# Mamba recurrence in a hybrid network: one more product with C on GpSimd, and the second step's input taken from SBUF

## The chip, the cores and the metric

The kernel runs on one core of a Trainium2 chip. The metric is the device time of one execution in microseconds, the median of several runs. The core has TensorE (PE in the profile, PEld for its weight loads), VectorE (DVE), ScalarE (ACT), GpSimd (POOL), and SyncE (SP), which issues most of the DMAs here. Each engine works through its own queue of instructions.

## What is computed

A batch of one image, 64 x 64 positions (4096 tokens) with 256 channels, goes through two layers: first a convolution and attention block, then a two-directional Mamba block with a small MLP, then a mixture of experts. The change lies in the Mamba part of the second layer. Its core, from the reference:

```python
dt = softplus(einsum('blr,dr->bld', dt, dt_proj_w) + dt_proj_b)
A = -exp(A_log)
dA = exp(dt[..., None] * A)
dBx = dt[..., None] * Bm[:, :, None, :] * xc[..., None]
def step(h, inp):
    dA_t, dBx_t, C_t = inp
    h = dA_t * h + dBx_t
    y = einsum('bds,bs->bd', h, C_t)
    return (h, y)
y = ys.transpose(1, 0, 2) + xc * Dp
y = y * silu(z)
return einsum('bld,ed->ble', y, out_proj_w)
...
fwd = _mamba(x, ...[0])
bwd = _mamba(x[:, ::-1, :], ...[1])
```

There are 512 inner channels with 16 states each, so 8192 recurrences over 4096 tokens in each direction.

## The kernel before, in words

`mamba_phase` cuts the tokens into 8 chunks of 512. A **step** i is one chunk in one direction, c, d = divmod(i, 2): even steps run forward, odd steps run backward (chunk 7 - c, read in reverse), so there are 16 steps. Step 1 works on chunk 7, which the attention phase leaves last; `start()` norms it into a tile `un`.

A step has 32 **slots** (`slots`, `SPS` = 32): four blocks e of 128 inner channels, in each four groups k of states, in each two halves j = 0 and 2. A slot handles 128 partitions x 2 x 512 elements. In the code n counts slots over all steps, and `at` = n % 32 is the place in the step. One slot takes these instructions:

- `inflow(n)` (L1726, GpSimd): dbx = dtxr times b. dtxr and dtr are tiles loaded by `load_dt` (L1473, SP) from a scratch in HBM, with each row broadcast; one pair serves four slots, and each has three buffers. dbx has three buffers too.
- `decay(n)` (L1716, ScalarE, two instructions): da = exp(dtr * A).
- `bring(n)` (L1764 on ScalarE, or L1762 on GpSimd at the places in `LONG`, which has 1): from step 2 on adds what the earlier chunk left to one column of dbx.
- `recur(n)` (L1739, VectorE): the scan, and then, unless the place is in `POOLED`, the product of the states with C (L1744, VectorE). At a place in `POOLED` the scan writes tile h directly, and `pooled(n)` does the product on GpSimd (L1749), issued one slot later.
- `keep(n)` (L1770, ScalarE): saves the last column as state.
- `sum_states(n)` (L1779, TensorE): for a pair of slots n and n + 1, four matmuls, each into its own strip of 32 partitions, add the products to y. At the first pair of a block a matmul with `skip` (L1777) opens y; the y tile has one buffer.
- `close(i, e)` (L1787, VectorE): after the last pair of a block, multiplies y with silu(z) into xc, and so frees y.

The order of the work is written by hand: the phase runs in `tc.manual_schedule`, and each engine's queue holds its instructions in the order in which the loop over slots issues them. In slot n the loop issues, in this order: a `carry` part at the places in `CARRY`, `inflow(n + 2)`, `keep(n - 1)`, `decay(n + 1)`, `bring(n + 1)`, `recur(n)`, loads, `pooled(n - 1)`, the sums that are due and `close`, then a step of `output(i - 1)` (L1488, matmuls that read what close wrote), the Silu of z at place 0 (L1854), a step of preparation, and a piece of a tail. So in slot 31 GpSimd gets the next step's inflow for place 1 and then, if 30 were in `POOLED`, the product of 30.

A pair is summed two slots after its first slot (j = 0). A pair whose first place is in `POOLED` = {4, 10, 12, 18, 28} is summed one slot later (j = 2). `close` of a block's last pair is issued in the first slot of the next block, right after that slot's scan and product.

The preparation of a step is a generator, `prepare(q)`, of 36 pieces: the input projection (L1300, reads u), copies out of PSUM (L1326 to L1334), the convolution in four groups (L1346, L1342), its Silu (L1350), the projection to dt, B and C (L1355 to L1361), softplus in several pieces (L1371 to L1395), the projection to z, and six pieces `dt_piece` on GpSimd that also store dt and dt * xc to HBM. Each slot issues one piece; the last five slots of a step (`AHEAD`) already begin with the step after the next. In step 0 another table, `LATE`, says how many pieces of `prepare(1)` each place issues, and `start()` still runs in its first slots. There step 1's input goes out to HBM (`ud[NCH - 1]`, L1631) and is loaded again by `load_u(1)` (L1309).

Of the kernel before, what the change touches and what calls it, by code (L numbers as in the profile page):

```python
# [1216 lines left out]
def mamba_phase(cx, early, w_in, w_x, w_out, w1, w2, x1d, ud, bcd, dtd, x2d, u2d, usum):  # L1217
# [12 lines left out]
    with ExitStack() as ctx:  # L1230
# [314 lines left out]
        def start():  # L1545


            got, xp = gots[0], early.xp
            x1 = tl.tile([P, CT, N], FP, name="x1", tag="a1b")
            nc.gpsimd.dma_start(out=x1, in_=x1d[NCH - 1])  # L1550
            un = tl.tile([P, CT, N], FP, name="un", tag="hn")
            norm = layer_norm(cx, tl, tl_psum, x1, un, nc.gpsimd)
            nc.scalar.copy(halo[0], xp[:, :, N : N + 3])
            xc = got["xc"] = pr.tile([P, ET, N], FP, name="xc", tag="xc")
            nc.scalar.activation(xc, xp[:, :, 0:N], AF.Silu)
            for d in range(2):
                nc.scalar.activation(aneg[d], cx.col(f"alog{d}", 0, ET * DS), AF.Exp)

                nc.vector.tensor_scalar(aneg[d], aneg[d], -1.0, -1e-30, ALU.mult, ALU.min)
            nx = DR + 2 * DS  # L1560
            pd = mm_psum()
            for e in range(ET):
                nc.tensor.matmul(pd[0:nx, :], wx[0][:, e, :], xc[:, e, :], start=e == 0, stop=e == ET - 1)
            xd = few()[0:nx, :]
            nc.scalar.copy(xd, pd[0:nx, :])
            nc.sync.dma_start(out=bcd[0], in_=xd[DR:nx, :])
            load_bc(0, 0)
            ex = early.wide("ex")[:, :, 0:N]
            dt = got["dt"] = sp.tile([P, ET, N], FP, name="dt", tag="dt")

            def soft(e):
                ps = mm_psum()
                nc.tensor.matmul(ps, wdt[0:DR, P * e : P * e + P], xd[0:DR, :], start=True, stop=True)
                nc.scalar.activation(ex[:, e, :], ps, AF.Abs, bias=cx.col("dtb0", e))
                nc.vector.tensor_scalar(dt[:, e, :], ps, cx.col("dtb0", e), 0.0, ALU.add, ALU.max)
                nc.scalar.activation(ex[:, e, :], ex[:, e, :], AF.Exp, scale=-1.0)

            def rest(e):

                rd = few()  # L1580
                nc.vector.tensor_scalar(rd, ex[:, e, :], -1.0, -1.0, ALU.mult, ALU.add)
                nc.vector.scalar_tensor_tensor(rd, rd, 1.0, ex[:, e, :], ALU.add, ALU.add)
                nc.vector.tensor_tensor(dt[:, e, :], dt[:, e, :], rd, ALU.add)

            def log(e):
                nc.scalar.activation(ex[:, e, :], ex[:, e, :], AF.Ln, bias=1.0)

            soft(0)
            rest(0)
            log(0)  # L1590
            for v in range(2):
                dt_piece(0, v, 0, ex, nc.vector)
            load_dt(0, 0, 0)
            load_dt(0, 0, 2)
            load_bc(0, 1)

            step(norm)
            step(norm)
            soft(1)
            step(norm)  # L1600
            soft(2)
            rest(1)
            soft(3)
            step(norm)
            inflow(0)
            decay(0)
            decay(1)
            rest(2)
            rest(3)
            step(norm)  # L1610
            load_bc(0, 2)
            zs = in_pair(0, ET)
            for e in range(1, ET):
                log(e)
            inflow(1)
            step(norm)
            load_bc(0, 3)
            yield

            for h in range(2):  # L1620
                z = sp.tile([P, 2, N], FP, name="z", tag="z", bufs=3)
                got.setdefault("z", []).append(z)
                for f in range(2):
                    nc.scalar.copy(z[:, f, :], zs[f])
                if h == 0:
                    zs = in_pair(0, ET + 2)
                    for v in range(2):
                        dt_piece(0, v, 1, ex)
                    yield
            step(norm)  # L1630
            nc.sync.dma_start(out=ud[NCH - 1], in_=un)  # L1631
            drain(norm)
            yield
            dt_piece(0, 0, 2, ex)
            yield
            dt_piece(0, 1, 2)
            yield
            for z in got["z"]:
                nc.scalar.activation(z, z, AF.Silu)
            dt_piece(0, 0, 3, ex)  # L1640
            load_u(1)
            yield
            dt_piece(0, 1, 3)
            yield
# [59 lines left out]
        SPS = ET * SQ * 2  # L1704
# [67 lines left out]
        def sum_states(n):  # L1772

            i, e, k, _ = slots[n]
            if k == 0:
                ys[i, e] = py.tile([P, N], FP, name="y", tag="y")
                nc.tensor.matmul(ys[i, e], skip[i % 2][:, e, :], gots[i]["xc"][:, e, :], start=True, stop=False)  # L1777
            for j in range(4):
                nc.tensor.matmul(  # L1779
                    ys[i, e][32 * j : 32 * j + 32, :], cx.sel, hs[n + j // 2][:, j % 2, :],  # L1780
                    start=False, stop=k == SQ - 1,
                )
            del hs[n], hs[n + 1]
# [6 lines left out]
        CARRY = {30: (0, 0), 31: (0, 2), 9: (1, 0), 11: (1, 2)}  # L1790


        POOLED = {4, 10, 12, 18, 28}

        AHEAD = 5

        LATE = {0: 0, 1: 0, 2: 0, 3: 0, 4: 0, 6: 2, 7: 6, 13: 2, 14: 2, 15: 2, 16: 2}
        LONG = {1, 9, 17, 24}

        FULL = {  # L1800
# [7 lines left out]
        with tc.manual_schedule(engines=ORDERED):  # L1808
# [5 lines left out]
            for n, (i, e, k, j) in enumerate(slots):  # L1814
                at = n % SPS
                if at == 0:
                    prep, coming = coming, None
                if at in CARRY and 1 < i + (at > 16) < 2 * NCH:
                    carry(i + (at > 16), *CARRY[at])
                inflow(n + 2)  # L1820
                if n > 0:
                    keep(n - 1)
                if n > 0:
                    decay(n + 1)
                bring(n + 1)
                recur(n)
                nxt = (i, e + 1) if e < ET - 1 else (i + 1, 0)
                if nxt[0] < 2 * NCH:
                    if e == ET - 1 and j == 0:
                        load_bc(i + 1, k)  # L1830
                    if (k, j) == (1, 2):
                        load_dt(*nxt, 0)
                    if (k, j) == (2, 2):
                        load_dt(*nxt, 2)
                if n > 0 and (n - 1) % SPS in POOLED:
                    pooled(n - 1)
                if j == 2 and n > 2 and (n - 3) % SPS in POOLED:
                    sum_states(n - 3)
                if j == 0 and n > 0:
                    if (n - 2) % SPS not in POOLED:  # L1840
                        sum_states(n - 2)
                    if k == 0:
                        close(*slots[n - 2][:2])
                        if e == 0:
                            out = output(i - 1)
                if 1 <= at <= 3 and out is not None:
                    step(out)
                    if at == 3:
                        out = None
                        if (i - 1) % 2:  # L1850
                            tails.append(tail((i - 1) // 2))
                if at == 0 and i > 0:
                    for z in gots[i]["z"]:
                        nc.scalar.activation(z, z, AF.Silu)  # L1854
                if i == 0:
                    step(begin)
                step(prep, LATE.get(at, 1) if i == 0 else 1)
                if at >= SPS - AHEAD and i + 2 < 2 * NCH:
                    coming = coming or prepare(i + 2)
                    step(coming)  # L1860
                if i > 0 and at in (2, 4):
                    dt_piece(i, 1, 2 if at == 2 else 3)
                if at == 1 and i > 1:
                    load_first(i, 1)
                elif at in (10, 30) and 1 < i + (at > 16) < 2 * NCH:
                    carry(i + (at > 16), at < 16, 1)
                if i == 2 * NCH - 1 and at in (26, 28):
                    ending = ending or last_output()
                    step(ending)
                if tails and (i == 2 * NCH - 1 or at not in FULL[needs[0]]):  # L1870
                    needs[0] = next(tails[0], None)
                    if needs[0] is None:
                        tails.pop(0)
                        needs[0] = "PE"
# [331 lines left out]
```

## Time and profile before

| what | value |
|---|---|
| median of 3 runs | 4168.57 us (4154.93 to 4173.5) |
| the profiled execution | 4163.05 us |
| its span, first to last instruction | 4160.9 us |
| mean granted TensorE clock | 0.923 |
| busy: PE, DVE, ACT, POOL | 3614.7, 3492.5, 2662.8, 1747.6 us |
| first scan of the Mamba recurrence to the last close | 1971.2 to 3837.9 us |
| step 0, first scan to the first scan of step 1 | 124.2 us |
| step 1 and 2, likewise | 110.5 and 114.2 us |
| steps 3 to 14, likewise | 113.5 to 119.1 us |

How to read it: a group's row on the page has line, engine, operation, output<-inputs, shapes and count, then busy time in us and mean of one in ns, then the idle time of that engine just before these instructions and what ended most of it. A timeline row has its start in us from the start of the span, its duration, engine, line and what it does; in brackets the idle time before it and its releaser. A row of the waits has who waited for whom, then the sum in us, the number of times, and the longest.

### The profile page before, as it was taken

The numbers are of one execution on the slowest core, as the hardware profiler recorded it, in microseconds if no ns is written. First come the engines' busy times: TensorE is split into PE (matmuls) and PEld (weight loads), VectorE is DVE, ScalarE is ACT, GpSimd is POOL, SyncE is SP. The second block draws the span as 40 slices with busy tenths as digits, with TensorE's granted clock in tenths as the row PEclk, the third lists the DMA queues.
The fourth block names the chain that finished last, engine by engine and source line by source line (L and its number), as shares of the span: only waits on it lengthen the run. The fifth ranks groups of instructions, "written<-read, shape, count | busy, mean of one in ns | idle before, by whom it ended". The sixth has DMA issues, their size and how long they took to land. (4 is left out here: it accounts for less than half of the span.)

```text
span 4160.9 us, 43567 instructions
## 1 busy us (share of the span) xinstructions
PE 3614.7 (87%) x15116; PEld 1185.4 (28%) x15116; DVE 3492.5 (84%) x2898; ACT 2662.8 (64%) x4131; POOL 1747.6 (42%) x1188
## 2 busy tenths in 40 slices
PE   6669789999999999998788788888888888876798
PEld 2223332222222222222222222222222222222343
DVE  8998867889889888778899999999999999998211
ACT  1111226878878878776777778778787877774122
POOL 3020000000000000001888889888898989896000
PEclk9889898999999999999888988998899999987899
DMA  6232124000000000002334344343334334341121
GB/s 207 91 110 94 56 71 135 12 27 19 19 21 19 19 22 19 11 22 86 110 117 126 121 126 129 117 133 112 125 115 124 120 122 141 108 137 64 66 67 39
DMA packets 150533, 351.20 MB, mean 84 GB/s; under 512 B 35493, under 2 KB 44453, under 8 KB 150046
## 3 DMA queue, kind: packets, MB, share of 16 engines
q1 hardware_dynamic: 139214, 313.17, 24.4%
q0 software_dynamic: 11088, 35.14, 2.4%
q8 instruction: 121, 1.98, 0.2%
q14 instruction: 110, 0.90, 0.1%
HBM read 268.69 MB, written 79.56 MB: 84 GB/s over the span
## 5 line engine op out<-in xcount | busy, mean ns | idle before, releaser
L1726 POOL TENSOR_TENSOR dbx<-dtxr,b 128x1024 f32<-128x1024 f32 x512 | 1202.1, 2358 | 192.9 <-DMA dtxr<-dtd 92.4
L1010 ACT ACTIVATE e<-sc 128x1024 f32<-128x1024 f32 x1024 | 992.9, 1023 | 203.4 <-PE sc L1003 160.3
L1739 DVE TENSOR_TENSOR_SCAN da<-da,state,dbx 128x1024 f32<-128x1024 f32 x432 | 1014.2, 2348 | 17.9 <-ACT da L1716 8.4
L929 DVE TENSOR_TENSOR s<-s,e 128x1024 f32<-128x1024 f32 x768 | 881.0, 1223 | 43.3 <-ACT e L1010 42.8
L1716 ACT ACTIVATE da<-dtr,aneg 128x512 f32<-128x512 f32 x1024 | 708.2, 692 | 33.2 <-DMA dtr<-dtd 3.3
L1003 PE MATMUL sc<-q,kS 32*128 32x512 f32 x4096 | 654.0, 643 | 11.7 <-ACT e L1010 7.8
L132 POOL TENSOR_TENSOR ln_few<-ln_few,minus_half 128x4 f32<-128x4 f32 x29 | 29.4, 1015 | 1408.1 <-DMA ln_few<-ln_row 1408.1
L1744 DVE TENSOR_TENSOR h<-da,c 128x1024 f32<-128x1024 f32 x432 | 529.2, 1225 | 34.0 <-PE y L1779 2.1
L936 PE MATMUL av<-e,vT 128*32 128x512 f32 x4096 | 548.7, 607 | 3.7 <-ACT o L942 3.7
L1779 PE MATMUL y<-h,sel 128*32 128x512 f32 x2048 | 373.2, 655 | 99.1 <-DVE h L1744 71.5
L453 PE MATMUL cv<-v,u 128*128 128x512 f32 x928 | 409.0, 600 | 28.0 <-DVE pad L274 14.3
L1300 PE MATMUL mm<-u,win 128*128 128x512 f32 x496 | 271.7, 699 | 88.1 <-ACT state L1770 29.1
L1003 PEld LDWEIGHTS sc<-q,kS 32*128 32x128 f32 x4096 | 211.7, 184 | 456.3 <-issue 229.8
L551 DVE SCALAR_TENSOR_TENSOR acc<-pad,wdw_s,acc 128x768 f32<-128x768 f32 (+1 forms) x192 | 235.9, 1234 | 25.6 <-ACT acc L544 20.0
L453 PEld LDWEIGHTS cv<-v,u 128*128 128x128 f32 x928 | 176.7, 192 | 258.4 <-issue 224.6
L1770 ACT COPY state<-da 128x2 f32<-128x2 f32 x431 | 68.0, 158 | 264.3 <-DVE h L1744 263.2
L1346 PE MATMUL mm<-xp,taps 128*128 128x512 f32 x480 | 213.2, 596 | 0.0
L929 DVE TENSOR_TENSOR s<-e 128x1024 f32<-128x1024 f32 x128 | 151.1, 1224 | 64.3 <-ACT e L1010 64.0
L1739 DVE TENSOR_TENSOR_SCAN h<-da,state,dbx 128x1024 f32<-128x1024 f32 x80 | 187.5, 2344 | 11.6 <-ACT state L1770 10.9
L936 PEld LDWEIGHTS av<-e,vT 128*32 128x32 f32 x4096 | 81.2, 108 | 396.4 <-issue 378.7
L1749 POOL TENSOR_TENSOR h<-h,c 128x1024 f32<-128x1024 f32 x80 | 188.4, 2355 | 2.1 <-ACT state L1770 2.1
L1300 PEld LDWEIGHTS mm<-u,win 128*128 128x128 f32 x496 | 106.2, 224 | 254.4 <-issue 109.8
(352 smaller groups left out, 3841.4 us busy)
## 6 DMA issues: line engine op xcount, KB each, us to landing
dtr<-dtd SPq DMA_DIRECT2D x128, 512.0 KB
dtxr<-dtd SPq DMA_DIRECT2D x128, 512.0 KB
b<-bcd SPq DMA_DIRECT2D x64, 256.0 KB
c<-bcd SPq DMA_DIRECT2D x64, 256.0 KB
dtd<-dt SPq DMA_DIRECT2D x64, 256.0 KB
dtd<-few SPq DMA_DIRECT2D x64, 256.0 KB
u<-uv SPq DMA_DIRECT2D x24, 640.0 KB
u<-ud SPq DMA_DIRECT2D x16, 512.0 KB
```

Source lines behind the costliest of these rows:

```text
L453: nc.tensor.matmul(rows4(ps), u[:, dy, P * ci : P * ci + P], v[:, dy : dy + HR, ci, :], start=dy + ci == 0, stop=dy == k - 1 and ci == CT - 1,
L551: nc.vector.scalar_tensor_tensor(o, src, w_ap, o, ALU.mult, ALU.add)
L929: nc.vector.tensor_tensor(z, x, y, ALU.add)
L936: nc.tensor.matmul(g.av[32 * h : 32 * h + 32, :], vT[:, kb, P * t + 32 * h : P * t + 32 * h + 32], es[h // 2][:, h % 2, :], start=kb == 0, ...
L1003: nc.tensor.matmul(ps[h // 2][:, h % 2, :], kS[r, t, P * kb : P * kb + P], q_t[r, t, :], start=True, stop=True,)
L1010: nc.scalar.activation(e, ps[i], AF.Exp)
L1300: nc.tensor.matmul(ps, win[d][:, t, P * e : P * e + P], u[:, t, ::-1] if d else u[:, t, :], start=t == 0, stop=t == CT - 1,)
L1716: nc.scalar.activation(da[:, v, :], dts[i, e, j][0][:, v, :], AF.Exp, scale=aneg[i % 2][:, a : a + 1])
L1726: nc.gpsimd.tensor_tensor(u, dts[i, e, j][1], bcs[i, k][0][:, None, :].to_broadcast([P, 2, N]), ALU.mult)
L1739: nc.vector.tensor_tensor_scan(das[n].rearrange("p v n -> p (v n)"), da.rearrange("p v n -> p (v n)"), u.rearrange("p v n -> p (v n)"), st ...
L1744: nc.vector.tensor_tensor(h, da, bcs[i, k][1][:, None, :].to_broadcast([P, 2, N]), ALU.mult)
L1779: nc.tensor.matmul(ys[i, e][32 * j : 32 * j + 32, :], cx.sel, hs[n + j // 2][:, j % 2, :], start=False, stop=k == SQ - 1,)
```

## The change

Step 1's input is taken from the tile `un` where the norm leaves it (`gots[1] = {"u": un}`), and `load_u(1)` goes. The store of that chunk to `ud` stays, since step 14 reads it. `LATE` starts `prepare(1)` at place 4 instead of 5; at places 4 to 16 the pieces lie up to two earlier or one later than before (16 issued by place 13 in both), and from place 17 on as before.

Place 30 joins `POOLED`: in every step, slot 30's product with C goes from VectorE to GpSimd. Its sum is not put off by a slot: where the first slot of a block (k == 0) is reached, the sum is issued at once, as `close` follows. The condition of the sums that are put off is written accordingly. In every sum the two strips of slot n + 1 are now added before those of slot n.

```diff
@@ start()
             norm = layer_norm(cx, tl, tl_psum, x1, un, nc.gpsimd)
+            gots[1] = {"u": un}
...
             dt_piece(0, 0, 3, ex)
-            load_u(1)
             yield
@@ sum_states(n)
-            for j in range(4):
+
+            for j in (2, 3, 0, 1):
                 nc.tensor.matmul(
                     ys[i, e][32 * j : 32 * j + 32, :], cx.sel, hs[n + j // 2][:, j % 2, :],
@@ tables
-        POOLED = {4, 10, 12, 18, 28}
+        POOLED = {4, 10, 12, 18, 28, 30}
...
-        LATE = {0: 0, 1: 0, 2: 0, 3: 0, 4: 0, 6: 2, 7: 6, 13: 2, 14: 2, 15: 2, 16: 2}
+        LATE = {0: 0, 1: 0, 2: 0, 3: 0, 5: 2, 6: 2, 7: 5, 15: 2, 16: 2, 17: 2}
@@ the loop over slots
-                if j == 2 and n > 2 and (n - 3) % SPS in POOLED:
+                if j == 2 and k > 0 and (n - 3) % SPS in POOLED:
                     sum_states(n - 3)
                 if j == 0 and n > 0:
-                    if (n - 2) % SPS not in POOLED:
+                    if k == 0 or (n - 2) % SPS not in POOLED:
                         sum_states(n - 2)
                     if k == 0:
                         close(*slots[n - 2][:2])
```

## The prediction

> **What bounds the kernel now.** I read the page first (busy times, then the groups), then the busy times by stretches of the Mamba phase (the recurrence, 1971 to 3840 us of the span), then the waits of each engine there, and last the timeline around a change of step. The page's groups give the price of one of each:
>
> ```profile
> L1726 POOL TENSOR_TENSOR dbx<-dtxr,b 128x1024 f32<-128x1024 f32 x512 | 1202.1, 2358 | 192.9 <-DMA dtxr<-dtd 92.4
> L1739 DVE TENSOR_TENSOR_SCAN da<-da,state,dbx 128x1024 f32<-128x1024 f32 x432 | 1014.2, 2348 | 17.9 <-ACT da L1716 8.4
> L1744 DVE TENSOR_TENSOR h<-da,c 128x1024 f32<-128x1024 f32 x432 | 529.2, 1225 | 34.0 <-PE y L1779 2.1
> L1749 POOL TENSOR_TENSOR h<-h,c 128x1024 f32<-128x1024 f32 x80 | 188.4, 2355 | 2.1 <-ACT state L1770 2.1
> ```
>
> 512 slots: each has one scan on VectorE (2.35 us); 432 have their product with C there (1.23), 80 on GpSimd (2.36). The stretches (columns: length, then busy time and count of PE, weight loads, VectorE, ScalarE, GpSimd, clock, DMA share, GB/s), each about one step of 32 slots:
>
> ```profile
> 2555.00:2670.00 115.00, 96.76 (x265) 31.31 (x268) 109.05 (x67) 90.95 (x180) 101.98 (x64) 0.88 0.40 120
> 3475.00:3590.00 115.00, 98.16 (x273) 31.96 (x274) 111.99 (x68) 94.35 (x186) 105.95 (x65) 0.88 0.40 122
> ```
>
> VectorE is busy 109 to 112 of 115 us, the rest is mostly gaps of some 0.03 to 0.1 us between instructions: it sets the step. GpSimd, at 102 to 106, is close behind. In its waits VectorE loses little; the largest are 14.1 us in step 0, from slot 5 to slot 16. The waits of 1970 to 2048 us say from where:
>
> ```profile
> DVE da L1739 <- ACT da L1716: 8.4, 4, 2.8
> DVE xc L1787 <- PE y L1779: 3.8, 2, 3.2
> PE mm L1300 <- DMA u<-ud: 7.0, 1, 7.0
> ```
>
> TensorE stands 7.0 us for step 1's input, then its work is late, ScalarE waits for it, and VectorE for ScalarE. The timeline where step 4 ends and step 5 begins:
>
> ```profile
> 2544.08 2.36 POOL L1749 TENSOR_TENSOR h<-h,c 128x1024 f32<-128x1024 f32 x1
> ...
> 2546.11 0.60 SPq L1473 DMA_DIRECT2D dtxr<-dtd  x1
> ...
> 2547.58 1.23 DVE L1744 TENSOR_TENSOR h<-da,c 128x1024 f32<-128x1024 f32 x1
> ...
> 2548.06 2.36 POOL L1726 TENSOR_TENSOR dbx<-dtxr,b 128x1024 f32<-128x1024 f32 x1
> ...
> 2551.17 1.23 DVE L1744 TENSOR_TENSOR h<-da,c 128x1024 f32<-128x1024 f32 x1
> ...
> 2552.45 1.05 PE L1779 MATMUL y<-h,sel 128*32 128x512 f32 x4 [1.11 <-DVE h L1744]
> 2552.50 2.36 POOL L1726 TENSOR_TENSOR dbx<-dtxr,b 128x1024 f32<-128x1024 f32 x1 [1.90 <-DVE h L1744]
> ...
> 2554.75 1.23 DVE L1744 TENSOR_TENSOR h<-da,c 128x1024 f32<-128x1024 f32 x1
> 2554.94 0.19 POOL L1762 TENSOR_TENSOR dbx<-dbx,brought 128x1 f32<-128x1 f32 x1
> 2555.08 6.99 POOL L1726 TENSOR_TENSOR dbx<-dtxr,b 128x1024 f32<-128x1024 f32 x3
> ...
> 2555.89 0.68 DVE L1787 TENSOR_TENSOR xc<-y,z 128x512 f32<-128x512 f32 x1
> 2556.49 2.35 DVE L1739 TENSOR_TENSOR_SCAN da<-da,state,dbx 128x1024 f32<-128x1024 f32 x1
> ```
>
> The first line is slot 28's product on GpSimd. The product of slot 30 is VectorE's at 2547.58, that of 31 at 2551.17. GpSimd's inflow for slot 0 of step 5 runs at 2548.06, that for slot 1 only at 2552.50: its tile dtxr was asked for at 2546.11, 6.4 us earlier. (The trace names a VectorE product as releaser; but this inflow's buffer was read last by slot 30's scan, long over, so I take the tile's landing.) At 2555.89 close (L1787) takes y, before the scan of slot 1.
>
> **What the Trainium skill says.** "PSUM — Partial Sum Buffer", Engine vs sequencer instructions: the queues of ScalarE, VectorE and GpSimdE are strictly first in, first out. The trace agrees: every inflow and product stands in the order of the code. "GPSIMD Engine Reference", 4.1 Engine selection: an elementwise operation of two inputs is about half as fast there; here 2355 against 1225 ns, 1.92 times. "ScalarE: Activation LUTs", What ACT_TABLE_LOAD costs: about 1283 ns for the load, and a drain of 1380; the trace has the 1.28 us, but the Silu at 2026.05 starts 1.29 us after its load's start at 2024.76, so no drain is counted.
>
> **The change, part by part.**
>
> 1. Slot 30's product leaves VectorE in 16 steps. A slot with product takes 3.59 us from scan to scan (2548.72 to 2552.32 is 3.60), one without 2.26 (2539.36 to 2541.62); I count 1.25 to 1.3, so at most 16 x 1.3 = 21 us.
>
> 2. What the same product does on GpSimd. pooled(30) is issued in slot 31, after that slot's inflow(n + 2), which is the one for slot 1 of the next step, and its bring (L1762). So it starts not when slot 30's scan ends (about 2547.5) but after 2555.1. Its sum isn't put off by a slot as those of the other five are: close comes at once. On VectorE close stands ahead of the scans of the whole next step, so they wait for the product. End of the product = end of inflow(1) + 0.24 (L1762 and gaps; none into step 1) + 2.36. Then 1.2 us to close: 1.06 for a sum on TensorE and two hand-overs (in step 0 a sum starts at 2009.03 and close at 2010.18). For step 5: 2554.86 + 0.24 + 2.36 + 1.2 = 2558.7, against 2555.89 before and 2554.64 with the gain of 1.25: VectorE stands 4.0 us and close is 2.8 us later than before. To the scan of slot 2 it is 0.61 + 3.59 us: 2562.9. Before it ran at 2560.39, after 0.28 us for ScalarE, which is no longer late then. So 2.5 us are lost. The same sum for all 15 changes of step, into step 1, 2, ... 15, from the trace's inflow, close and slot 2 scan: 0.0, 4.2, 4.2, 3.6, 2.5, 2.5, 1.2, 3.4, 1.4, 0.4, 3.3, 2.1, 2.8, 3.9, -0.1: together **+35.4 us**, the saving on VectorE already taken off. Where inflow(1) waited for nothing (steps 1, 10, 15) the loss is 0 to 0.4; elsewhere it waited 0.8 to 5.1. I take it that these repeat: from slot 23 on GpSimd runs without a pause (2520.55 to 2550.6, 0.2 us idle), released by a load that follows VectorE's pace.
>
> 3. The last slot 30 has no inflow behind it: its 2.36 us lie beside slot 31's scan and product (3.57): -1.3 us.
>
> 4. GpSimd after the change of step: 2.36 us later, VectorE as late, so no new wait there: 0. TensorE holds behind the sum of slot 30 the output's first three matmuls (L1488), which now run before close (2553.43, 2.84 us). It comes out at product's end + 6.8 (sum and hand-over 1.15, L1488 3.6, skip 1.0, slot 0's sum 1.05) = 2564.3, before 2561.2: 3.1 us later, VectorE 2.5. Its conv and ScalarE's Silu behind that gave waits of 1.3 to 1.6 us at slot 12 of steps 5, 6, 8, 10, 12 and 14. Between 0 and 0.6 a step; I take 0.2: +3.
>
> 5. Step 0. The norm's last multiply leaves `un` at 2.34 us from 1979.84, 1982.2; the copy out to ud and load_u(1) (issued 1990.27, used 1994.3) fall from the way of TensorE, which can start after its sum at 1987.3: 7 us sooner. By hand through the new LATE: the wait of 2.77 at slot 8 goes; close of slot 8 still waits, since two conv groups (3.7 us each) stand before its sum, and comes near 2007.3 for 2010.18; Silu moves to slot 11, in front of the decay of slot 13, while slot 12 has only its scan: some 3.5 us for the 2.40 there before; the 2.36, 0.86 and 0.56 at slots 14 to 16 go; one step more of ScalarE work in 15 to 17 may bring 1.5 back. Left: **-4**. Bounds: 0, and -12.2 (all but the 1.95 at slots 5 and 6, which the z Silu makes). SP has one issue (0.39 us) less; its queue isn't late there. `un` lies in a buffer that the next tail takes two steps later: 0.
>
> 6. The order 2, 3, 0, 1 in a sum: the product that may be late is used last. A sum takes about 1.05 us whether 2 or 4 of its matmuls are left (the x4 and x8 rows): 0; if four late ones cost 0.9 more (one sum took 1.9) at the 6 closes that waited, +5. The two conditions move no other sum: the old five pairs are put off as before.
>
> Sum: 35.4 - 1.3 + 3 - 4 = +33 us. On the profiled execution, 4163.05 us (span 4160.9 and 2.15 around it), that is 4196; the median of the runs, 4168.57, lies 5.5 above it, which gives 4202. I say **4199**.
>
> **The rivals.** (a) Faster: the product is hidden. If GpSimd has finished inflow(1) 3.8 us before the new close, nothing waits: 16 x -1.3 - 4 = -25, 4138 to 4144. For it: VectorE is the bound and GpSimd has 9 us a step to spare. Against it: the best three changes of step still miss by 1.6 to 2.1 us (0.3 to 0.8 us lost at close, plus the 1.25). (b) No change: GpSimd's queue sets the close, but the loads land in time everywhere, as into steps 1, 10 and 15: 15 x 0.3 - 1.3 - 4 = -1, 4165. (c) Worse: TensorE, held behind the sum, makes conv, Silu and decay late, and each step loses 0.6 there instead of 0.2 and another 1.5 at slots 12 and 16, as several do now: 33 + 15 x 1.9 = 61, 4224 to 4230.
>
> **Chances.** Forecast 0.66, (a) 0.10, (b) 0.16, (c) 0.08. 0.5% (21 us; about what a measurement can tell from no change) ends at 4189: of the forecast's own range, 4178 to 4218 by the unknowns above, about 0.09 lies below. So faster 0.10, same 0.25, slower 0.65. The range 4163 to 4225 leaves out (a), a part of (b) and of (c).
>
> **What would show it.** L1744 x416 and L1749 x96; VectorE's wait at L1787 for y rises from 10.9 to some 65 us, about 4 at the first close of a step, with GpSimd's L1749 just before it, behind an L1726 that waited for dtxr; TensorE's 7.0 us on u<-ud gone and step 0 (124.2 us to the first scan of step 1) near 119. I am wrong if L1787's wait stays near 10, or if the steps from 1 on are 1.3 us shorter.

## The result, and the profile after

The changed kernel takes 4208.24 us, median of 4 runs (4202.44 to 4215.9); the kernel before, with one more run beside it, 4167.23. The medians differ by 41 us; the ratio on record, taken over the runs, is 1.0109, 95% interval 1.009 to 1.0128. The forecast was 4199, from a working that came to 33 us more. The profiled execution has a span of 4204.2 us.

The rows of the page that answer to those of before:

```profile
L1726 POOL TENSOR_TENSOR dbx<-dtxr,b 128x1024 f32<-128x1024 f32 x512 | 1203.2, 2359 | 196.5 <-DMA dtxr<-dtd 97.5
L1739 DVE TENSOR_TENSOR_SCAN da<-da,state,dbx 128x1024 f32<-128x1024 f32 x416 | 976.5, 2347 | 19.6 <-ACT dbx L1764 11.5
L1744 DVE TENSOR_TENSOR h<-da,c 128x1024 f32<-128x1024 f32 x416 | 509.6, 1225 | 31.0 <-PE y L1780 0.7
L1749 POOL TENSOR_TENSOR h<-h,c 128x1024 f32<-128x1024 f32 x96 | 226.0, 2355 | 1.4 <-ACT state L1770 1.4
```

Sixteen products moved, 1225 ns each on VectorE and 2355 on GpSimd. One scan (2347 ns) and one product on VectorE take as long as before (2348 and 1225), so the sixth product beside them doesn't slow them. VectorE's busy time on the page fell from 3492.5 to 3474.2 us, 18 us. It stands longer than that for something new. VectorE's waits of 1960 to 3890 us:

```profile
DVE xc L1788 <- PE y L1780: 65.3, 20, 9.2
DVE h L1739 <- ACT state L1770: 18.1, 19, 1.6
DVE da L1739 <- ACT dbx L1764: 11.5, 12, 1.7
```

`close` (now L1788) waits 65.3 us for y, where it waited 10.9. From VectorE's timeline, 56.2 of it is the first close of the steps 1 to 15, which had no wait before. The timeline at the same change of step as before, step 4 to 5, with the releaser in brackets. The first line is slot 28's product, the next the issue of the load that slot 1's inflow waits for, the third slot 30's scan:

```profile
2563.77 2.37 POOL L1749 TENSOR_TENSOR h<-h,c 128x1024 f32<-128x1024 f32 x1
...
2564.80 0.60 SPq L1473 DMA_DIRECT2D dtxr<-dtd  x1
2564.81 2.34 DVE L1739 TENSOR_TENSOR_SCAN h<-da,state,dbx 128x1024 f32<-128x1024 f32 x1
...
2567.77 2.37 POOL L1726 TENSOR_TENSOR dbx<-dtxr,b 128x1024 f32<-128x1024 f32 x1
...
2571.06 2.35 POOL L1726 TENSOR_TENSOR dbx<-dtxr,b 128x1024 f32<-128x1024 f32 x1 [0.74 <-DMA dtxr<-dtd]
...
2573.13 1.23 DVE L1744 TENSOR_TENSOR h<-da,c 128x1024 f32<-128x1024 f32 x1
...
2573.49 0.19 POOL L1762 TENSOR_TENSOR dbx<-dbx,brought 128x1 f32<-128x1 f32 x1
2573.63 2.35 POOL L1749 TENSOR_TENSOR h<-h,c 128x1024 f32<-128x1024 f32 x1
...
2576.04 1.57 PE L1780 MATMUL y<-h,sel 128*32 128x512 f32 x4 [4.21 <-POOL h L1749]
...
2577.54 4.83 PE L1488 MATMUL mm<-xc,wout 128*128 128x512 f32 x8
2577.65 0.69 DVE L1788 TENSOR_TENSOR xc<-y,z 128x512 f32<-128x512 f32 x1 [3.29 <-PE y L1780]
```

Slot 30's scan ends at 2567.15. Its product starts at 2573.63, behind two inflows and a bring; the second inflow waited for its dtxr tile, asked for at 2564.80. The sum on TensorE waits 4.21 us for the product, close 3.29 us for the sum, and close stands before the scan of slot 1. Each wait is charged to the engine just before it; the first cause lies further back, in what stands ahead of the product in GpSimd's queue. At this change of step most of the delay is the two inflows and what else GpSimd had before them, and the load adds 0.74 us; at the change from step 2 to 3 the second inflow waited 6.3 us for its load.

### The profile page after: what moved, and what is told of

Same layout as the page of the kernel before. It is cut to its first block, busy times and chain, and to the rows that moved or that the text cites. A ratio compares the mean times of both kernels' runs of the same rounds, so it can differ in the third digit from the quotient of the medians.

```text
span 4204.2 us, 43522 instructions
## 1 busy us (share of the span) xinstructions
PE 3602.9 (86%) x15116; PEld 1185.8 (28%) x15116; DVE 3474.2 (83%) x2882; ACT 2661.5 (63%) x4131; POOL 1786.3 (42%) x1204
## 5 line engine op out<-in xcount | busy, mean ns | idle before, releaser
L1739 DVE TENSOR_TENSOR_SCAN da<-da,state,dbx 128x1024 f32<-128x1024 f32 x416 | 976.5, 2347 | 19.6 <-ACT dbx L1764 11.5
L1716 ACT ACTIVATE da<-dtr,aneg 128x512 f32<-128x512 f32 x1024 | 708.2, 692 | 46.4 <-DVE h L1739 12.6
L1744 DVE TENSOR_TENSOR h<-da,c 128x1024 f32<-128x1024 f32 x416 | 509.6, 1225 | 31.0 <-PE y L1780 0.7
L1780 PE MATMUL y<-h,sel 128*32 128x512 f32 x2048 | 341.3, 668 | 175.2 <-DVE h L1744 96.8
L1300 PE MATMUL mm<-u,win 128*128 128x512 f32 x464 | 249.9, 688 | 76.4 <-ACT z L1407 26.0
L1739 DVE TENSOR_TENSOR_SCAN h<-da,state,dbx 128x1024 f32<-128x1024 f32 x96 | 225.0, 2344 | 18.8 <-ACT state L1770 18.1
L1749 POOL TENSOR_TENSOR h<-h,c 128x1024 f32<-128x1024 f32 x96 | 226.0, 2355 | 1.4 <-ACT state L1770 1.4
L1770 ACT COPY state<-da 128x2 f32<-128x2 f32 x415 | 65.3, 157 | 245.1 <-DVE h L1744 244.0
L1780 PEld LDWEIGHTS y<-h,sel 128*32 128x32 f32 x2048 | 48.6, 112 | 420.5 <-DVE h L1744 181.6
```

What stands on the lines that cost most here:

```text
L1300: nc.tensor.matmul(ps, win[d][:, t, P * e : P * e + P], u[:, t, ::-1] if d else u[:, t, :], start=t == 0, stop=t == CT - 1,)
L1716: nc.scalar.activation(da[:, v, :], dts[i, e, j][0][:, v, :], AF.Exp, scale=aneg[i % 2][:, a : a + 1])
L1739: nc.vector.tensor_tensor_scan(das[n].rearrange("p v n -> p (v n)"), da.rearrange("p v n -> p (v n)"), u.rearrange("p v n -> p (v n)"), st ...
L1744: nc.vector.tensor_tensor(h, da, bcs[i, k][1][:, None, :].to_broadcast([P, 2, N]), ALU.mult)
L1780: nc.tensor.matmul(ys[i, e][32 * j : 32 * j + 32, :], cx.sel, hs[n + j // 2][:, j % 2, :], start=False, stop=k == SQ - 1,)
```

## The experiments

All ratios are to the kernel before on the same chip, with their intervals. My theory (1): the product is late because it stands behind an inflow that waits for its load, and close stands behind the product. The rivals: (2) GpSimd has no room for a sixth product; (3) the new order within the sums costs; (4) the step 0 part disturbs the later steps.

**One part at a time.** First the step 0 part alone:

```diff
+            gots[1] = {"u": un}
...
-            load_u(1)
...
-        LATE = {0: 0, 1: 0, 2: 0, 3: 0, 4: 0, 6: 2, 7: 6, 13: 2, 14: 2, 15: 2, 16: 2}
+        LATE = {0: 0, 1: 0, 2: 0, 3: 0, 5: 2, 6: 2, 7: 5, 15: 2, 16: 2, 17: 2}
```

> The kernel before with the step 0 part alone: un as step 1's input, no load_u(1), the new LATE; POOLED and the sums as before. My theory: step 0 is 4 to 6 us shorter (118 to 120 us from its first scan to that of step 1, 124.2 before), nothing else moves: about 4162, some 5 us under the kernel before; the wait at close in slot 0 of the steps stays near zero. Rival (the step 0 part shifts the later steps): steps 1 to 15 longer, over 4175.

4154.95 us, ratio 0.9993 (0.9983 to 1.0004). Step 0 took 120.0 us instead of 124.2; steps 1 to 14 took 116.1 us on average, before 115.9. So in the profile this part takes some 4 us off step 0 and leaves the later steps as they were, and rival (4) falls; the time as a whole can't be told from that of the kernel before.

Then the other part alone, the changed kernel with that diff undone:

> The changed kernel without its step 0 part: load_u(1) and the old LATE, un not used as input; place 30 and the new order in the sums stay. My theory: step 0 about 124 us from its first scan to that of step 1 where the changed kernel has 118.6; the rest as in the changed kernel with 50 to 60 us at close in slot 0: 3 to 6 us over the changed kernel, 1.011 to 1.013 times the kernel before. Rival: the two parts act on each other (the early preparation makes the later steps slow): under 1.005.

4200.42 us, 1.0097 (1.0075 to 1.0118); step 0 took 125.9 us, and the first closes waited 52.4 us. The loss is there without the step 0 part. The 3 to 6 us that this part was expected to save don't show: the medians even differ the other way, and each of the two ratios is uncertain by 8 or 9 us.

Then the changed kernel with the old order of the strips:

```diff
-            for j in (2, 3, 0, 1):
+            for j in range(4):
```

> The changed kernel with the strips of a sum added in the old order 0, 1, 2, 3. Theory 1: the order costs nothing, within 5 us of the changed kernel (1.009 to 1.012 times the kernel before), with 50 to 60 us at close in slot 0. Theory 3 (the new order costs): under 1.005.

4206.89 us, 1.0125 (1.0105 to 1.0146), 57.5 us at the first closes. Without the new order the loss is as large, so the order isn't what costs; whether it gains a little can't be told, since the intervals overlap. Rival (3) falls.

**Take away the load's wait.** The inflow for slot 1 reads the earlier dtxr tile. The values of slot 1 are wrong then; what is looked at is the time:

```diff
-                u, dts[i, e, j][1], bcs[i, k][0]...
+                u, dts[i, e, 0 if n % SPS == 1 else j][1], bcs[i, k][0]...
```

> The changed kernel, but the inflow for slot 1 of every step reads the dtxr tile of the first half (loaded two slots earlier), so it computes slot 1 from wrong rows and doesn't wait for the later tile; all else as in the changed kernel. If the DMA wait of that inflow is what makes the product late (about 34 of the 60 us that I worked out), the wait at close in slot 0 falls from 56 us to 20 to 30 and the time to some 4180. If it is GpSimd's queue alone, the wait stays over 45 and the time over 4198. If the DMA wait is all of it, the wait falls under 10.

4173.45 us, 1.0039 (1.0025 to 1.0053). VectorE's waits again:

```profile
DVE xc L1788 <- PE y L1780: 34.3, 17, 2.9
```

24.9 us of that are first closes, where the changed kernel had 56.2. So 31.3 us, somewhat over half of the wait, are the load, where some 34 had been expected, and the rest comes with GpSimd's queue: two inflows stand before the product even when nothing is awaited.

**Take the product out from behind the inflow.** My first edit put it at the head of slot 31:

```diff
+                if at == 31:
+                    pooled(n - 1)
                 inflow(n + 2)
...
-                if n > 0 and (n - 1) % SPS in POOLED:
+                if n > 0 and at != 31 and (n - 1) % SPS in POOLED:
                     pooled(n - 1)
```

> The changed kernel, but in slot 31 GpSimd gets slot 30's product ahead of the inflow for the next step's slot 1. Theory 1 (the product stands behind an inflow that waits for its DMA, and close behind the product): the wait at close in slot 0 falls from 56 us in 15 steps to under 10; of the 1.3 us a step that VectorE saves most is taken back at slot 2, where ScalarE is only 0.3 us early, so the time is 0 to 15 us under the kernel before, 4150 to 4165. Theory 2 (a sixth product is too much for GpSimd, wherever it stands): the inflows are late instead, and the time stays over 4190. Theory 3 (the new order within the sums costs): stays over 4190 as well, with waits at close of slots 8, 16 and 24.

4195.42 us, 1.0088 (1.0071 to 1.0105): missed. The timeline at a change of step, with ScalarE's keep of slot 30 in the middle:

```profile
2560.32 2.37 POOL L1749 TENSOR_TENSOR h<-h,c 128x1024 f32<-128x1024 f32 x1
...
2562.71 0.20 ACT L1770 COPY state<-h 128x2 f32<-128x2 f32 x1 [4.59 <-POOL h L1749]
...
2564.54 2.36 DVE L1739 TENSOR_TENSOR_SCAN da<-da,state,dbx 128x1024 f32<-128x1024 f32 x1 [3.72 <-ACT dbx L1764]
```

The wait at the first closes was gone, but the product, which overwrites h in place, now stood ahead of keep as well, which reads h (and so saved the product as the state). So ScalarE's queue waited for GpSimd, the decay behind it was late, and slot 0's scan waited 46.6 us in 15 steps, slot 2's 16.4. The edit had made waits of the same size elsewhere. It tells nothing against theory 1. The next kernel issues keep first:

```diff
+                if at == 31:
+                    keep(n - 1)
+                    pooled(n - 1)
                 inflow(n + 2)
-                if n > 0:
+                if n > 0 and at != 31:
                     keep(n - 1)
...
-                if n > 0 and (n - 1) % SPS in POOLED:
+                if n > 0 and at != 31 and (n - 1) % SPS in POOLED:
                     pooled(n - 1)
```

> As e3 (slot 30's product ahead of the inflow for slot 1 on GpSimd), but behind ScalarE's keep of slot 30, as elsewhere; in e3 the product stood ahead of keep too, so that keep waited for it and copied the product for the state. Theory 1 (product behind a waiting inflow, close behind the product): no wait over 0.5 us at slot 0, neither at the scan nor at close; left are the waits for ScalarE that e3 shows, 1.1 us at slot 2 in each step and 1.06 at slot 31 in some, so the time is 0 to 10 us under the kernel before. Theory 2 (no room on GpSimd): over 1.005 times the kernel before.

4144.57 us, 0.9967 (0.9954 to 0.998): 0.3% faster than the kernel before, and so faster than both. GpSimd's timeline at the change from step 5 to 6:

```profile
2654.96 0.23 POOL L1455 TENSOR_TENSOR brought<-brought,state 128x16 f32<-128x16 f32 x1
2655.14 2.36 POOL L1749 TENSOR_TENSOR h<-h,c 128x1024 f32<-128x1024 f32 x1
2657.45 2.37 POOL L1726 TENSOR_TENSOR dbx<-dtxr,b 128x1024 f32<-128x1024 f32 x1
```

and VectorE's there:

```profile
2660.17 1.22 DVE L1744 TENSOR_TENSOR h<-da,c 128x1024 f32<-128x1024 f32 x1
2661.31 0.68 DVE L1788 TENSOR_TENSOR xc<-y,z 128x512 f32<-128x512 f32 x1
2661.90 2.35 DVE L1739 TENSOR_TENSOR_SCAN da<-da,state,dbx 128x1024 f32<-128x1024 f32 x1
```

The product runs ahead of the inflow, which finds its load landed afterwards (here and at nine more of the 15 changes); it is done at 2657.50, and close comes only at 2661.31. Over all 15 changes of step the first closes waited 1.3 us, where the changed kernel had 56.2. The same six products, the same engines, one exchange in a queue: from 1.0109 to 0.9967. Waits of 4.0 us at slot 0, 3.9 at slot 1 and 5.7 at slot 2 remain over 15 steps, more of them than the expectation had.

**Leave GpSimd's order and put close off.** The sum of slots 30 and 31 and close are issued in slot 1:

```diff
+                if at == 1 and n > 1:
+                    sum_states(n - 3)
+                    close(*slots[n - 3][:2])
+                    out = output(i - 1)
-                if j == 0 and n > 0:
-                    if k == 0 or (n - 2) % SPS not in POOLED:
+                if j == 0 and n > 0 and at > 0:
+                    if (n - 2) % SPS not in POOLED:
...
-                        if e == 0:
-                            out = output(i - 1)
```

> The changed kernel, but the sum of slots 30 and 31 and close of the last block are issued in slot 1 of the next step instead of slot 0; GpSimd's order is that of the changed kernel. Theory 1: VectorE gets slot 1's scan and product (3.6 us) in front of close, so of the waits of 2 to 9 us at close some 10 to 15 us in all remain of 56; with 1 us at slot 2 in each step for ScalarE the time is about that of the kernel before, within 10 us. If the loss came from GpSimd being late in general, the next inflows would be late too and the time would stay over 1.007 times the kernel before.

4195.37 us, 1.0086 (1.0066 to 1.0106): missed by some 35 us. VectorE's waits:

```profile
DVE da L1739 <- ACT dbx L1764: 31.6, 31, 2.9
DVE h L1739 <- ACT state L1770: 21.5, 21, 1.5
DVE xc L1788 <- PE y L1780: 12.6, 12, 2.1
DVE m L1495 <- PE mm L1488: 12.4, 12, 1.6
```

The wait at close fell from 65.3 to 12.6 us as meant, and most of that came back at scans of slots 5, 7 and 10 and at the output's additions. TensorE's and ScalarE's waits, one line each, say where it went:

```profile
PE y L1780 <- POOL h L1749: 75.1, 25, 7.6
```

```profile
ACT xc L1342 <- PE mm L1346: 96.2, 60, 2.8
```

TensorE's queue still waits for the product (75.1 us; 77.8 in the changed kernel, 27.4 before, 23.5 in e8). Behind that sum stand the output's matmuls and the next convolution, so ScalarE waits for the convolution (96.2 us; 71.1 in the changed kernel, 35.8 before, 28.6 in e8), and the decay behind that is late for VectorE. In this kernel the late product costs nearly as much through TensorE's queue as it did through VectorE's. This is the path of the forecast's rival (c): TensorE, held behind the sum, makes convolution and decay late. That the waits follow from one another in this way is read from the two queues; no run takes one of them out alone.

**Other places for the sixth product.** Place 20 and then place 24 instead of 30 in the changed kernel:

```diff
-        POOLED = {4, 10, 12, 18, 28, 30}
+        POOLED = {4, 10, 12, 18, 20, 28}
```

> The changed kernel with place 20 in POOLED instead of 30: six products a step on GpSimd as in the changed kernel, none of them next to a change of step. Theory 1: no wait at close in slot 0; 16 x 1.25 us saved on VectorE and some 5 in step 0, about 4142 (4138 to 4155). Theory 2 (GpSimd has no room for a sixth product): over 4185.

4163.51 us, 1.0011 (1.0002 to 1.002). No wait at the first closes, so not rival (2) at this place; but no gain either. The timeline shows where it went, slots 20 and 21 of step 5:

```profile
2612.37 2.34 DVE L1739 TENSOR_TENSOR_SCAN h<-da,state,dbx 128x1024 f32<-128x1024 f32 x1
...
2614.74 1.42 ACT L1716 ACTIVATE da<-dtr,aneg 128x512 f32<-128x512 f32 x2 [0.69 <-DVE h L1739]
...
2616.41 2.36 DVE L1739 TENSOR_TENSOR_SCAN da<-da,state,dbx 128x1024 f32<-128x1024 f32 x1 [1.70 <-ACT dbx L1764]
```

The decay for slot 21 starts when slot 20's scan is over, and then takes 1.42 us and the bring 0.28; slot 20 has no product on VectorE to cover them. 1.7 us in 13 steps and 1.54 in two more (25.2 us in all) is more than the 1.25 us a step that VectorE saves.

> The changed kernel with place 24 in POOLED instead of 30, which has no other place of POOLED two slots away; as many products on GpSimd as in the changed kernel. Theory 1: no wait at close in slot 0 and none like that of e4 at slot 21, so most of the 20 us saved on VectorE stays: 0.993 to 0.998 of the kernel before. Theory 2 (GpSimd has no room in slots 24 to 31, where it runs without pause): inflows late there, over 1.003.

4174.01 us, 1.0031 (1.0016 to 1.0046): missed. Over steps 1 to 15 there are 18.1 us of waits at slot 0's scan, 13.6 at slot 25's, 12.0 at slot 2's. Two causes mix here. From about slot 23 on GpSimd runs almost without pause, and 2.36 us more there make the inflow for slot 0 late: in the steps whose scan of slot 0 waits longest, over 2 us, that inflow ends only 0.5 us before the scan. So rival (2) holds for this stretch: by its busy share GpSimd has room, but not between slots 24 and 31, except in the gap before the inflow of slot 1, which e8 uses. The wait at slot 25 is not of that kind. As at slot 21 in e4, ScalarE's decay starts only when the scan before it is over, here slot 24's, while GpSimd's inflow for slot 25 had ended by then; and here it came after a single slot without a product on VectorE.

Last, e8 with place 26 for 28, so that no two of the last places are two slots apart:

> As e8 (product of slot 30 ahead of the inflow, behind keep), with place 26 in POOLED for 28. In the changed kernel and in e4 a scan waited 1.06 to 1.7 us where two places of POOLED lie two slots apart, since ScalarE's decay comes only when the second scan is over. Theory: with 26 and 30 that wait at slot 31 (5.3 us in all) goes, nothing else moves: 0 to 6 us under e8, 0.9955 to 0.9970 of the kernel before. If the product of 26 meets GpSimd's dt pieces of slots 25 to 28 badly, loads and inflows come later and it is slower than e8, over 0.9975.

4142.77 us, 0.9956 (0.9942 to 0.997). The wait at slot 31's scan fell from 5.3 to 1.8 us over 15 steps. It is as fast as e8 or a little faster, the intervals overlap; both beat the kernel before and the changed one.

## Why the prediction was right, by its steps

The direction, the place and the mechanism held; the size, +33, was short of +41. In the profiles the Mamba phase, first scan to last close, grew from 1866.7 to 1908.7 us, +42.0.

1. **VectorE's saving** was put at most at 21 us; its busy time fell by 18.3. Right.
2. **The late product.** The stands at close were worked out as 60.5 us in all, 4.0 of them at step 5. The trace has 56.2 at the first closes, 3.29 of them at step 5, and 8.1 more just ahead of them: 5.3 at slot 31's scan and 2.8 at slot 0's, which the forecast didn't have. These lie between slot 30's scan and close, and in each of these steps close still waits after them, so they took their time from the wait at close. Together 64.3, 3.8 more than forecast. One error made it larger: from the product's end to close it was not 1.2 us but 1.15 to 2.02, 8.2 more over the 15 changes. It was 1.15 in the four where the sum took 1.05 us; in the other eleven TensorE's granted clock fell to 0.50 and the sum took 1.57 to 1.92. Part 6 of the working had weighed this (+5) and put it at 0. The other way went 4.4 us: inflow(1) ended 1.6 us sooner after slot 30's scan in sum, and the rest is in small pieces. So the agreement of the whole wait at `close`, 65.3 us for some 65, is in part luck. e6 and e8 show both links.
3. **The last slot 30** is part of point 1 and can't be seen alone.
4. **TensorE behind the sum** is the other mis-sized term. It was put at +3 us; the waits at slots 10 and 12, where the convolution's lateness arrives, rose from 11.5 to 18.1, +6.7. The working had TensorE come out 3.1 us later but left its speed unchanged; the L1488 group took 4.83 us there, where 3.70 is usual (2584.16, the next such group).
5. **Slot 31's scan** waits 1.06 us in each of five steps. Places 28 and 30 both have only a scan, and in these steps ScalarE's decay for slot 31 starts only when slot 30's scan is over; with 26 for 28, in e9, the wait fell from 5.3 to 1.8 us. Why it is these five steps alone the traces don't tell. The forecast had seen the same between slots 12 and 13 in step 0 and didn't apply it to 28 and 30. In the changed kernel it costs little, since close waits anyhow.
6. **Step 0**: forecast -4; -4.2 in e1. Of its waits, those at slots 14 to 16 went, and 2.16 us at slot 19 came, about as worked out by hand.

The forecast's 33, with 8.2 for the slower sums, -4.4 for products that were less late, 3.7 at slots 10 and 12 and a wait of 1.7 at one slot 5, comes to 42.2, and the profiles have 42.0. So what the forecast lacked is for the most part that TensorE was slower after it had waited.

## What to carry to other kernels

When work moves to an engine that has time to spare, ask at which place in its queue it will stand, what that queue waits for there, and which in-order queues hold the reader: the busy share says nothing on any of the three. A late producer blocks every queue that holds one of its readers, so putting off one reader, as e5 did, only hands the wait to the next; what helps is to move the producer ahead of the instruction that waits, after checking who else reads the tile that it overwrites. A slot relieved of its product can outrun the engine that feeds the next one: it did where two such slots lay two apart, and in e10 after one alone.

## What the runs showed of the hardware

TensorE is slower for a while after it has stood still. The same group of eight L1300 records in the changed kernel, after a shorter and after a longer idle time:

```profile
2563.77 3.70 PE L1300 MATMUL mm<-u,win 128*128 128x512 f32 x8 [2.05 <-ACT xp L1328]
```

```profile
2804.59 5.40 PE L1300 MATMUL mm<-u,win 128*128 128x512 f32 x8 [3.17 <-ACT xp L1328]
```

Over the Mamba phase of both kernels all 12 such groups after 0.7 to 2.12 us of idle took 3.67 to 3.70 us, and all 40 after 2.68 us or more took 5.17 to 6.72. But the length of the idle time alone doesn't decide it. One of the sums behind the late product, in the changed kernel:

```profile
3533.98 1.05 PE L1780 MATMUL y<-h,sel 128*32 128x512 f32 x4 [3.64 <-POOL h L1749]
```

Over this sum and the group behind it (3533.98 to 3538.80) the granted clock in the trace was 1.00. In the trace's record of that clock, the changed kernel's Mamba phase has 83 spells at 0.50. All begin on one grid of 3.41 us and last one to six of its periods, and no period at full clock in which TensorE was busy for less than 0.4 of the time was followed by another at full clock. So an idle time seems to count by how it lies on this grid: the 3.64 us above lie across two periods. This is read from the records; no run tests it. The Trainium skill, "TensorE: Matmul & The Clock Gate", Part 1: The HAM clock gate, tells of a clock that falls to half after an idle window of about 3.4 us. The half and the 3.4 us agree; as the length of one idle time in the profile the 3.4 us can't be taken, since 2.68 us before a group were followed by half clock and these 3.64 us were not.

What a wait costs TensorE beyond itself: after 4.21 us for the product of step 4, the next sum took 1.57 us instead of 1.05, and the group after it 4.83 instead of 3.70.

Why ScalarE's decay for slot 21 in e4 starts only at the end of slot 20's scan, though its buffer was last used by slot 19, the trace doesn't tell; the same holds for slot 25 in e10. This stays open.
